# Token-sum stores on GpSimd's queue, the second batch's routing steps earlier, and up-factors through the fill buffers

## The chip, the cores and the metric

The kernel runs on one core of a Trainium2 chip. The metric is the device time of one execution in microseconds (us). The kernel is written with a tile framework: the source fixes the order of instructions on TensorE (PE), VectorE (DVE), ScalarE (ACT) and GpSimd (POOL) as it is written, and the framework orders the DMA issues of SyncE (SP) by a planner's due times. Every engine works through its own queue in order, so an instruction that waits holds up all behind it on its engine.

## The reference

Two batches of 1024 tokens with 1024 features go through a layer norm. A block-sparse linear layer (mask of 32 x 32 blocks) gives s. A LoRA mixture gives g: a plain linear layer, plus eight low-rank pairs weighted by a softmax that depends on the mean token of the batch. The output is x + s * g.

```python
xn = _layernorm(x)
s = einsum('bsk,nk->bsn', xn, weight * block_mask) + bias
base = einsum('bsi,oi->bso', xn, W_org)
q = einsum('bi,ki->bk', xn.mean(axis=1), Wq)
coeffs = softmax(einsum('bk,ek->be', q, lora_keys) / sqrt(128))
delta = einsum('be,bser,ero->bso', coeffs, einsum('bsi,eir->bser', xn, lora_down), lora_up)
out = x + s * silu(base + delta)
```

## The kernel before

Every float32 operand of a product is split in a high part (a cast on ACT) and a low part (a subtraction on DVE), and each product is three matmuls: high x high, high x low, low x high. A 128 x 512 output tile of a full-depth product is 24 matmuls (`gemm`, L425 to L427).

The order of work is this. Batch 0: the S product's first half, then the Y weights are made and the Y product's first half runs (phase `y00`), then its second half (phase `y01`, tiles 0 to 7, jobs in `jobs_c`). Then a stretch of *folds*: the Y weights of batch 1 are made by 16 folds (one per half and k tile) and stored to DRAM (`yu`), with the eight S tiles of batch 0's second half (`s_tile`) between them: 4, 4, 3, 3, 2 folds after S tiles 0 to 4. Last, batch 1's products are done by a Strassen-like scheme (`quad`, L1131), whose operand sums were prepared before.

A **fold** (`fold`) makes one 128 x 512 block of W_org^T + down x (coefficients * up). It loads `ds` (a down block) and `wo` (a W_org block) for the next fold (`y_prep`, L375 and L377), splits ds into `dhi` (ACT, L380) and `dlo` (DVE, L381), runs 12 matmuls into `psw` (`y_mul`, L389 to L391) and adds `wo` (DVE, L396). The scaled up-factors are the four `cut` tiles of one half: `scale_up(b, h)` loads four `us` tiles (L364), and multiplies each by the coefficients on ACT (L367, high) and DVE (L368, low). The second half's factors, `scale_up(1, 1)`, are made at the end of fold 7.

The **routing** of batch 1, `coeffs(1)`, gives four steps. steps[0] spreads the token sums by eight TensorE transposes (L297); steps[1] is the query (DVE, L321 and L325); steps[2] is the scores: a pair of small matmuls (L332), DVE's L334 to L337, and the exponential as a power on POOL (L339); steps[3] is the softmax's sum and division (DVE, L345 to L352), which gives the coefficients `c`. In the kernel before, jobs_c runs steps[0] and steps[1] after the seventh tile of y01 and its S weight, and the other two with `scale_up(1, 0)` after the eighth tile and its S weight.

Also in `jobs_c`: an S weight block per tile (`s_mul`: load of `ws`, L272, mask product on DVE, L274, cast on ACT, L277; `s_lo`: DVE, L282). S tile 0 needs the eighth of these blocks for its last three matmuls. And the **token sums** of batch 1: for each of four groups j, `wide_a` and `wide_b` normalize a block on DVE and form seven sums, which are stored to DRAM (`xv`), five DMAs a group: `ac` and `bd` of 512 KB, three more of 256 KB. They are put in `late_stores`, and `store_late` issues all that wait there from ACT's queue (L480); jobs_c calls it once a tile, between `s_mul` and `s_lo`.

A **fill** (`fill`, L984 to L986) loads one of these sums back into one third of `misc` (three buffers in turn, which held the query weights until steps[1] had read them), and splits it into `xw`, the operands of `quad`. Before, a fill follows the second and the fourth fold after S tiles 0 and 1.

Buffers that matter: `stage` has six 128 x 512 places, shared by ws, us, ds, wo and some sums; `cu` has five of 128 x 2 x 512, shared by the wide blocks of the sums and the cut tiles; `res` has three, each held until the output store that reads it has landed.

Of the kernel before, what the change touches and what calls it, by code (L numbers as in the profile page):

```python
# [9 lines left out]
F32 = mybir.dt.float32  # L10
# [7 lines left out]
P = 128  # L18
# [3 lines left out]
NKT = D // P  # L22
NH = 512
# [9 lines left out]
def kernel(  # L33
# [26 lines left out]
    nc = tc.nc  # L60
# [23 lines left out]
    stage = for_fold("stage", 2)  # L84
# [16 lines left out]
    misc = c0pool.tile([P, 3, NH], F32, name="misc")  # L101
# [254 lines left out]

    cu = {}

    def scale_up(b, h):
        cu[(b, h)] = []  # L360
        for c in range(4):
            t = cupool.tile([P, 2, NH], F32R, name="cut", tag="cu")
            st = stage.tile([P, NH], F32, name="us", tag="st", bufs=6)
            nc.sync.dma_start(st, up[c * P : (c + 1) * P, h * NH : (h + 1) * NH])  # L364
            s = csel[b][:, c : c + 1]
            hi = t[:, 0, :]
            nc.scalar.activation(hi, st, AF.Copy, scale=s)  # L367
            nc.vector.scalar_tensor_tensor(  # L368
                t[:, 1, :], st, s, hi.bitcast(F32), ALU.mult, ALU.subtract
            )  # L370
            cu[(b, h)].append(t)

    def y_prep(b, h, kt):
        ds = stage.tile([P, 4, P], F32, name="ds", tag="st", bufs=6)
        nc.sync.dma_start(ds, down[kt])  # L375
        ws = stage.tile([P, NH], F32, name="wo", tag="st", bufs=6)
        nc.sync.dma_start(ws, worgT[kt * P : (kt + 1) * P, h * NH : (h + 1) * NH])  # L377
        dhi = stage.tile([P, 4, P], F32R, name="dhi", bufs=2)
        dlo = stage.tile([P, 4, P], F32R, name="dlo", bufs=2)
        nc.scalar.copy(dhi, ds)  # L380
        nc.vector.tensor_tensor(dlo, ds, dhi.bitcast(F32), ALU.subtract)  # L381
        staged[(b, h, kt)] = dhi, dlo, ws

    def y_mul(b, h, kt):
        dhi, dlo, ws = staged[(b, h, kt)]
        u = cu[(b, h)]
        ps = ps_w.tile([P, NH], F32, name="psw", tag="psw")
        for c in range(4):
            nc.tensor.matmul(ps, lhsT=dhi[:, c, :], rhs=u[c][:, 0, :], start=c == 0, stop=False)  # L389
            nc.tensor.matmul(ps, lhsT=dhi[:, c, :], rhs=u[c][:, 1, :], start=False, stop=False)  # L390
            nc.tensor.matmul(ps, lhsT=dlo[:, c, :], rhs=u[c][:, 0, :], start=False, stop=c == 3)  # L391
        staged[(b, h, kt)] = ps, ws

    def y_sum(b, h, kt):
        ps, ws = staged[(b, h, kt)]
        nc.vector.tensor_tensor(ws, ws, ps, ALU.add)  # L396
# [18 lines left out]
    def open_gemm(b, i, w, c0=0, n=NH):  # L415

        ps = ps_acc.tile([P, NH], F32, name="acc_ps", tag="acc_ps")[:, :n]
        g, j = divmod(i, 4)
        xs = xg[(b, g)]
        cols = slice(j * P, (j + 1) * P)  # L420
        wc = slice(c0, c0 + n)

        def part(k0, k1):
            for kt in range(k0, k1):
                nc.tensor.matmul(ps, lhsT=xs[:, kt, 0, cols], rhs=w[:, kt, 0, wc], start=kt == 0, stop=False)  # L425
                nc.tensor.matmul(ps, lhsT=xs[:, kt, 0, cols], rhs=w[:, kt, 1, wc], start=False, stop=False)  # L426
                nc.tensor.matmul(ps, lhsT=xs[:, kt, 1, cols], rhs=w[:, kt, 0, wc], start=False, stop=kt == NKT - 1)  # L427

        return ps, part

    def gemm(b, i, w, c0=0, n=NH):
        ps, part = open_gemm(b, i, w, c0, n)
        part(0, NKT)
        return ps
# [40 lines left out]
    late_stores = []  # L475

    def store_late():

        while late_stores:
            nc.scalar.dma_start(*late_stores.pop(0))  # L480

    pending = []

    def flush():
        while pending:
            pending.pop(0)()

    def phase(kind, b, h, w, final, jobs):

        for i in range(TPB):  # L490
            t = b * TPB + i
            if final:
                res = stage_l.tile([P, NH], F32, name="res", tag="res", bufs=3)
                nc.sync.dma_start(res, x[t * P : (t + 1) * P, h * NH : (h + 1) * NH])
            flush()
            ps = gemm(b, i, w)
            if final:
                pending.append(J(final_evac, kind, b, h, i, ps, res))
            else:
                pending.append(J(tile_evac, kind, b, h, i, ps))  # L500
            for job in jobs(i):
                job()

    J = lambda f, *a: (lambda: f(*a))
# [98 lines left out]
    with tc.manual_schedule(engines={mybir.EngineType.PE, mybir.EngineType.DVE, mybir.EngineType.Activation, mybir.EngineType.Pool}):  # L603
# [256 lines left out]
        xv = dram.tile([4, P, 7, NH], F32, name="xv")  # L860
# [36 lines left out]
        def wide_norm(j, half):  # L897
            t = wide[j][2 * half]
            nc.vector.tensor_tensor(t, t, rows["mean"], ALU.subtract)
            nc.vector.scalar_tensor_tensor(  # L900
                t, t, 1.0, rows["rstd"], ALU.mult, ALU.mult, accum_out=xsum[:, j + 4 * half : j + 4 * half + 1]
            )

        def sub(o, a, b):
            nc.vector.tensor_tensor(o, a, b, ALU.subtract)

        def fresh():
            return stage.tile([P, NH], F32, name="xt", tag="st", bufs=6)
# [4 lines left out]
        def wide_b(j):  # L913

            wide_norm(j, 1)
            ac, (t1, t2), bd = wide[j]
            sub(t1, ac[:, 1], ac[:, 0])
            sub(t2, bd[:, 1], t1)
            sub(ac[:, 1], bd[:, 1], ac[:, 1])
            t4 = stash_p.tile([P, NH], F32, name="t4", tag="stash") if j == 0 else fresh()  # L920
            sub(t4, bd[:, 0], t2)
            late_stores.append((xv[j, :, 0:2, :], ac))
            late_stores.append((xv[j, :, 2:4, :], bd))
            for k, t in ((4, t1), (5, t2), (6, t4)):
                late_stores.append((xv[j, :, k, :], t))

        phase("y", 0, 0, y00, True, jobs_b)


        s1 = new_slot()  # L930
        steps = coeffs(1)

        def jobs_c(i):
            yield J(s_mul, s1, 1, i)
            yield J(store_late)
            yield J(s_lo, s1, 1, i)
            if i in (1, 3):
                yield J(wide_load, (i + 3) // 2, 0)
                yield J(wide_load, (i + 3) // 2, 1)
            if i < 6:  # L940
                yield J((wide_a, wide_b)[i % 2], 1 + i // 2)
            if i == 6:
                yield steps[0]
                yield steps[1]
            if i == 7:
                yield steps[2]
                yield steps[3]
                yield J(scale_up, 1, 0)

        phase("y", 0, 1, y01, False, jobs_c)  # L950


        folds = [(h, kt) for h in range(2) for kt in range(NKT)]

        def fold(n):
            h, kt = folds[n]
            if n + 1 < len(folds):
                y_prep(1, *folds[n + 1])
            store_late()
            y_mul(1, h, kt)  # L960
            flush()
            y_sum(1, h, kt)
            ps, ws = staged.pop((1, h, kt))
            late_stores.append((
                yu[:, :, 2 * h + kt // 4, kt % 4, :].rearrange("u p n -> p u n"),
                ws.rearrange("p (u n) -> p u n", n=P),
            ))
            if n == NKT - 1:
                scale_up(1, 1)

        xw = {}
        XV = (0, 2, 3, 4, 5, 1, 6)
# [15 lines left out]
        spare = []  # L988
        ORDER_X = (0, 3, 4, 1, 5, 2, 6)

        def s_tile(i):
            res = stage_l.tile([P, NH], F32, name="res", tag="res", bufs=3)
            nc.sync.dma_start(res, x[i * P : (i + 1) * P, NH:])
            store_late()
            flush()
            ps = gemm(0, i, s1)
            pending.append(J(final_evac, "s", 0, 1, i, ps, res))
# [6 lines left out]
        def unit_load(u, i):  # L1004
            kind, p = units[u]
            src = wu[p] if kind == "s" else yu[p].rearrange("p a j n -> p (a j n)")
            c = slice(2 * i * NH, 2 * (i + 1) * NH)
            nc.sync.dma_start(raw_flat[:, c], src[:, c])
# [45 lines left out]
        def fills(j, n):  # L1054
            for _ in range(n):
                fill(j, ORDER_X[filled[j]])
                filled[j] += 1

        for i, n in enumerate((4, 4, 3, 3, 2)):
            s_tile(i)  # L1060
            for k in range(n):
                fold(done)
                done += 1
                if i < 3 and (i == 2 or k in (1, 3)):
                    fills(0, 1)
                if i > 2 and (i == 4 or k):
                    fills(1, 1)
                if i in (2, 3):
                    early.pop(0)()
            if i == 0:  # L1070
                unit_load(0, 0)
                unit_load(0, 1)
# [198 lines left out]
```

## Time and profile before

| What | us |
|---|---|
| median of three runs | 464.17 (461.12 to 466.78) |
| the profiled execution's own time | 465.36 |
| its span, first to last instruction | 463.6 |
| mean granted TensorE clock | 0.982 of full speed |

The page divides the span in 40 slices. The row for the granted TensorE clock and that of the DMA engines' busy share are, in tenths:

```profile
PEclk9799999999999999997999999999999999999998
DMA  8995506587862497887878885754364237209103
```

A slice is 11.6 us, so y01 with its jobs is in slices 15 to 18, and the folds follow to slice 25. An engine's idle time costs something only where that engine sets the pace. A row of a group is read as: line, engine, operation, output <- inputs, count | busy us, mean ns of one | idle before it and who ended it. A releaser is inferred from semaphore events.

### The profile page before, as it was taken

Reading aid. Unit: us, or ns where it says so; the run is one execution under the profiler, and the core shown is the slowest. Engines: PE = TensorE matmul, PEld = TensorE weight load, DVE = VectorE, ACT = ScalarE, POOL = GpSimd, SP = SyncE. Lnnn points to the kernel's source line nnn. Section 1 sums busy time; section 2 is a strip of 40 time slices with the busy share of each in tenths; the row PEclk is TensorE's granted clock in tenths of the full one; section 3 lists DMA queues with packets and bytes.
Section 4 is the critical chain, followed back from the end, with each engine's and each line's share of the span. In section 5 each row is a group of like instructions: output and inputs, shape, how many; then the busy total and the mean of one; then the engine's idle time right before and its main releaser. Section 6 shows DMA issues by size and latency. Waiting matters only on the chain.

```text
span 463.6 us, 5733 instructions
## 1 busy us (share of the span) xinstructions
PE 446.5 (96%) x2047; PEld 366.5 (79%) x2047; DVE 304.8 (66%) x492; ACT 169.3 (37%) x277; POOL 48.6 (10%) x52
## 2 busy tenths in 40 slices
PE   7799999999999999996999899999999999999995
PEld 5689888888887888885888688877888888888884
DVE  6879778666775788856555875868474385455624
ACT  3566725354323132213314223248343332431510
POOL 3755310000010000001000000000030020002000
PEclk9799999999999999997999999999999999999998
DMA  8995506587862497887878885754364237209103
GB/s 268 391 326 190 165 24 198 187 258 254 303 229 92 166 324 263 285 294 257 259 224 265 249 286 169 249 176 149 106 136 138 90 93 181 90 13 209 51 1 113
DMA packets 48173, 89.52 MB, mean 193 GB/s; under 512 B 4752, under 2 KB 14992, under 8 KB 48144
## 3 DMA queue, kind: packets, MB, share of 16 engines
q1 hardware_dynamic: 32784, 70.28, 45.7%
q10 hardware_dynamic: 13632, 15.73, 10.0%
q0 software_dynamic: 1728, 3.15, 4.6%
q8 instruction: 16, 0.26, 0.2%
q14 instruction: 13, 0.11, 0.1%
HBM read 69.21 MB, written 19.92 MB: 192 GB/s over the span
## 4 chain that ended last, share of the span: by engine, by line
PE 76%; DVE 11%; DMA 6%; ACT 2%; issue 2%; ACTq 1%; POOL 0%; SPq 0%; DVEq 0%
PE acc_ps L1131 23%; PE py L1131 9%; PE acc_ps L427 8%; PE acc_ps L425 8%; PE acc_ps L426 8%; PE psw L391 6%; PE psw L389 6%; PE psw L390 6%; DMA ws<-in_wT_dram 3%; DMA raw<-in_x_dram 1%; DVE slot L544 1%; ACTq L480 1%; DMA us<-in_up_dram 1%; DMA xv<-bd 1%; DVE ws L274 1%
## 5 line engine op out<-in xcount | busy, mean ns | idle before, releaser
L1131 PE MATMUL acc_ps<-xw,ow 128*128 128x512 f32 x480 | 113.8, 393 | 0.4 <-ACT acc_ps L1162 0.4
L426 PE MATMUL acc_ps<-slot,xgrp 128*128 128x512 f32 (+1 forms) x288 | 106.9, 371 | 2.7 <-DVE slot L544 2.7
L425 PE MATMUL acc_ps<-slot,xgrp 128*128 128x512 f32 (+1 forms) x288 | 107.6, 374 | 0.1
L427 PE MATMUL acc_ps<-slot,xgrp 128*128 128x512 f32 (+1 forms) x288 | 106.6, 370 | 0.7 <-DVE xgrp L556 0.7
L1131 PEld LDWEIGHTS acc_ps<-xw,ow 128*128 128x128 f32 x480 | 90.0, 188 | 21.4 <-ACT acc_ps L1162 0.9
L426 PEld LDWEIGHTS acc_ps<-slot,xgrp 128*128 128x128 f32 x288 | 55.4, 192 | 12.2 <-DVE slot L544 3.6
L427 PEld LDWEIGHTS acc_ps<-slot,xgrp 128*128 128x128 f32 x288 | 55.3, 192 | 10.2 <-DVE xgrp L556 1.1
L425 PEld LDWEIGHTS acc_ps<-slot,xgrp 128*128 128x128 f32 x288 | 55.3, 192 | 9.1 <-DVE stash L439 0.3
L389 PE MATMUL psw<-cut,dhi 128*128 128x512 f32 x128 | 51.5, 403 | 3.8 <-ACT dhi L380 3.7
L391 PE MATMUL psw<-cut,dlo 128*128 128x512 f32 x128 | 51.4, 401 | 1.5 <-DVE dlo L381 1.5
L390 PE MATMUL psw<-cut,dhi 128*128 128x512 f32 x128 | 51.0, 398 | 0.0
L1131 PE MATMUL py<-xw,ow 128*128 128x512 f32 x192 | 46.9, 392 | 0.0
L1131 PEld LDWEIGHTS py<-xw,ow 128*128 128x128 f32 x192 | 36.1, 188 | 8.1
L1031 DVE TENSOR_TENSOR ow<-raw,ow 128x1024 fp32r<-128x1024 f32 (+1 forms) x32 | 34.5, 1088 | 9.8 <-ACT ow L1030 9.6
L380 ACT CAST dhi<-ds 128x512 fp32r<-128x512 f32 x32 | 19.8, 617 | 42.5 <-PE psw L390 22.6
L396 DVE TENSOR_TENSOR wo<-wo,psw 128x512 f32<-128x512 f32 x32 | 21.9, 685 | 17.1 <-PE psw L391 17.0
L389 PEld LDWEIGHTS psw<-cut,dhi 128*128 128x128 f32 x128 | 24.7, 193 | 9.7 <-ACT dhi L380 4.1
L1114 POOL DMA_DIRECT2D gate<-in_xT_dram x12 | 10.8, 932 | 199.9 <-DVE gate L1112 130.8
L391 PEld LDWEIGHTS psw<-cut,dlo 128*128 128x128 f32 x128 | 24.7, 193 | 8.2 <-DVE dlo L381 2.8
L1030 ACT CAST ow<-raw 128x1024 fp32r<-128x1024 f32 (+1 forms) x32 | 29.4, 940 | 2.0 <-DVE xw L986 2.0
L390 PEld LDWEIGHTS psw<-cut,dhi 128*128 128x128 f32 x128 | 24.8, 193 | 5.4
L381 DVE TENSOR_TENSOR dlo<-ds,dhi 128x512 fp32r<-128x512 f32 x32 | 21.9, 686 | 9.0 <-ACT dhi L380 9.0
(152 smaller groups left out, 450.0 us busy)
## 6 DMA issues: line engine op xcount, KB each, us to landing
ds<-in_down_dram SPq DMA_DIRECT2D x32, 256.0 KB, 3.5
wo<-in_worgT_dram SPq DMA_DIRECT2D x32, 256.0 KB, 3.8
raw<-in_x_dram SPq DMA_DIRECT2D x11, 512.0 KB, 5.9
res<-in_x_dram SPq DMA_DIRECT2D x16, 256.0 KB, 3.3
us<-in_up_dram SPq DMA_DIRECT2D x16, 256.0 KB, 3.7
out_dram<-res ACTq DMA_DIRECT2D x16, 256.0 KB, 2.9
raw<-in_wu_dram SPq DMA_DIRECT2D x8, 512.0 KB, 5.2
yu<-wo ACTq DMA_DIRECT2D x16, 256.0 KB, 3.7
```

The costliest lines, as they stand in the source:

```text
L380: nc.scalar.copy(dhi, ds)
L381: nc.vector.tensor_tensor(dlo, ds, dhi.bitcast(F32), ALU.subtract)
L389: nc.tensor.matmul(ps, lhsT=dhi[:, c, :], rhs=u[c][:, 0, :], start=c == 0, stop=False)
L390: nc.tensor.matmul(ps, lhsT=dhi[:, c, :], rhs=u[c][:, 1, :], start=False, stop=False)
L391: nc.tensor.matmul(ps, lhsT=dlo[:, c, :], rhs=u[c][:, 0, :], start=False, stop=c == 3)
L396: nc.vector.tensor_tensor(ws, ws, ps, ALU.add)
L425: nc.tensor.matmul(ps, lhsT=xs[:, kt, 0, cols], rhs=w[:, kt, 0, wc], start=kt == 0, stop=False)
L426: nc.tensor.matmul(ps, lhsT=xs[:, kt, 0, cols], rhs=w[:, kt, 1, wc], start=False, stop=False)
L427: nc.tensor.matmul(ps, lhsT=xs[:, kt, 1, cols], rhs=w[:, kt, 0, wc], start=False, stop=kt == NKT - 1)
L1030: nc.scalar.copy(o[:, a:b, 0], raw[:, a:b])
L1031: nc.vector.tensor_tensor(o[:, a:b, 1], raw[:, a:b], o[:, a:b, 0].bitcast(F32), ALU.subtract)
L1131: nc.tensor.matmul(ps, lhsT=o[:, a, wl, j, :], rhs=xw[j][:, m, xl, :], start=start and j == 0 and k == 0, stop=j == 3 and k == 2, skip_gro ...
```

## The change

1. The token-sum stores get a list of their own, `sum_stores`, which `store_sums` issues from POOL's queue directly after the sums of a group are formed. `jobs_c` no longer calls `store_late`; what is left in late_stores then (the last output tile of y00) goes out at the first fold.
2. steps[0] and steps[1] run ahead of the seventh S weight. steps[2] is put inside the last tile of y01, after four of its eight k steps (`split_at`). steps[3] and `scale_up(1, 0)` run ahead of the eighth S weight.
3. `scale_up(1, 1)` takes the three thirds of misc for three of its four loads; the turn of misc (`spare`) advances by three.
4. The second fill after S tiles 0 and 1 follows the third fold in place of the fourth.

In the built programs this moves on SP: the load of the eighth S weight behind the four loads of up-factors and two fill loads; the res load of S tile 2 from y01 to behind the fourth fold's loads; three of the second half's up-factor loads up to 8 places ahead of their old place, and three fill loads behind them. On ACT the 20 sum stores are gone; the eighth S weight's cast is behind the four L367. On DVE the eighth S weight's two operations are behind the four L368. On POOL the 20 stores stand between the last L152 and L339.

```diff
-    def scale_up(b, h):
+    def scale_up(b, h, homes=()):
         cu[(b, h)] = []
         for c in range(4):
             t = cupool.tile([P, 2, NH], F32R, name="cut", tag="cu")
-            st = stage.tile([P, NH], F32, name="us", tag="st", bufs=6)
+            st = homes[c] if c < len(homes) else stage.tile([P, NH], F32, name="us", tag="st", bufs=6)
...
+    sum_stores = []
+
+    def store_sums():
+
+        while sum_stores:
+            nc.gpsimd.dma_start(*sum_stores.pop(0))
+
+    split_at = {}
...
-            ps = gemm(b, i, w)
+            if (b, h, i) in split_at:
+                ps, part = open_gemm(b, i, w)
+                part(0, 4)
+                split_at[(b, h, i)]()
+                part(4, NKT)
+            else:
+                ps = gemm(b, i, w)
...
-            late_stores.append((xv[j, :, 0:2, :], ac))
-            late_stores.append((xv[j, :, 2:4, :], bd))
+            sum_stores.append((xv[j, :, 0:2, :], ac))
+            sum_stores.append((xv[j, :, 2:4, :], bd))
             for k, t in ((4, t1), (5, t2), (6, t4)):
-                late_stores.append((xv[j, :, k, :], t))
+                sum_stores.append((xv[j, :, k, :], t))
+            store_sums()
...
         def jobs_c(i):
+            if i == 6:
+                yield steps[0]
+                yield steps[1]
+            if i == 7:
+                yield steps[3]
+                yield J(scale_up, 1, 0)
             yield J(s_mul, s1, 1, i)
-            yield J(store_late)
             yield J(s_lo, s1, 1, i)
...
-            if i == 6:
-                yield steps[0]
-                yield steps[1]
-            if i == 7:
-                yield steps[2]
-                yield steps[3]
-                yield J(scale_up, 1, 0)
-
+
+        split_at[(0, 1, 7)] = steps[2]
         phase("y", 0, 1, y01, False, jobs_c)
...
             if n == NKT - 1:
-                scale_up(1, 1)
+                homes = [misc[:, (len(spare) + k) % 3, :] for k in range(3)]
+                spare.extend(homes)
+                scale_up(1, 1, homes)
...
-                if i < 3 and (i == 2 or k in (1, 3)):
+                if i < 3 and (i == 2 or k in (1, 2)):
                     fills(0, 1)
```

## The prediction

> **What bounds the kernel now.** I read the page's busy shares first, then PE's list of waits, then the table by stretches, then the chain of waits around each hole.
>
> ```profile
> PE 446.5 (96%) x2047; PEld 366.5 (79%) x2047; DVE 304.8 (66%) x492; ACT 169.3 (37%) x277; POOL 48.6 (10%) x52
> ```
>
> TensorE is the bound: 96% busy. From 150 to 210 us every 10 us stretch shows PE fully busy, so nothing the change moves there can gain by itself. Only holes can be won. PE's waits name two after 150 us that the change can reach:
>
> ```profile
> PE psw L389 <- ACT dhi L380: 3.7, 1, 3.7
> PE psw L391 <- DVE dlo L381: 1.5, 1, 1.5
> ```
>
> What each hole costs beyond the wait is in the stretches (busy PE, PEld, DVE, ACT, POOL, then the granted clock, DMA share, GB/s):
>
> ```profile
> 210.00:215.00 5.00, 2.12 (x10) 1.42 (x8) 2.37 (x7) 2.35 (x4) 1.65 (x1) 1.00 0.51 177
> 215.00:220.00 5.00, 4.23 (x10) 3.03 (x11) 3.49 (x6) 1.92 (x4) 0.00 (x0) 0.52 0.87 300
> 220.00:230.00 10.00, 10.00 (x41) 8.17 (x40) 5.40 (x9) 3.10 (x5) 0.00 (x0) 0.90 0.81 257
> 250.00:260.00 10.00, 8.28 (x35) 6.02 (x35) 8.49 (x13) 5.10 (x9) 0.00 (x0) 1.00 0.77 226
> ```
>
> After the first hole the clock is 0.52: matmuls follow each other every 0.43 us instead of 0.2275 until 222. After the second, shorter hole it stays 1.00. The first, in PE's own rows:
>
> ```profile
> 211.73 0.39 PE L427 MATMUL acc_ps<-slot,xgrp 128*128 128x512 f32 x1
> 215.77 0.79 PE L389 MATMUL psw<-cut,dhi 128*128 128x512 f32 x1 [3.65 <-ACT dhi L380]
> ...
> 222.07 0.39 PE L391 MATMUL psw<-cut,dlo 128*128 128x512 f32 x1
> ```
>
> At 0.2275 the first fold matmul would start at 211.96 and the 15th at 215.15; it starts at 222.07. **Hole one costs 6.92 us**: 3.81 of idling, 3.11 of half clock. For hole two I count starts from 254.40 to 260.19: 15 steps, 3.41 us at full pace, 5.79 taken: **2.38 us**. The chain of waits (start, length, what) tells why hole one exists:
>
> ```profile
> 202.39 0.70 DVE ws L274
> 203.12 0.33 ACT slot L277
> 203.49 0.57 ACTq L480
> 204.10 0.64 ACTq L480
> 204.78 1.18 ACTq L480
> 206.00 1.49 ACTq L480
> ...
> 208.12 0.62 ACT slot L277
> 208.76 0.69 DVE slot L282
> ...
> 210.07 1.66 POOL ex L339
> ```
>
> ACT issues the last five sum stores (L480) from 203.13 to 207.5, with SP's loads in flight (302 GB/s over 195 to 212). They hold up the cast L277 of the last S weight; DVE's L282 behind it holds up the scores; these give POOL's exponential, the coefficients, the factor casts L367 (212.65) and at last dhi.
>
> **The change, part by part** (line numbers of the kernel before).
>
> *Stores on POOL.* The 20 issues leave ACT; POOL has nothing else between 137 and 210. Only the fourth group stands in front of POOL's exponential. Nearest price: POOL's other DMA, L1114, mean 932 ns, 880 median. A store of 512 KB has as many packets: ACT's five stores of that window are 721 packets, 144 each, as the 12 gate DMAs have (1728/12). So five times 0.93: from 199.45 (the DVE row that finishes ac) POOL is busy to 204.1. [...] The row: the L1114 at 343.25 takes 0.87 us and lies inside a 1.23 us DVE L1031. DVE beside the stores has the same kind, two-input f32 operations, so I take 0.93. [...] From below: it can't be under 0.87 each, the shortest row.
>
> *Routing ahead.* steps[0] and steps[1] now precede the seventh S weight. PE's transposes for them sit at 199.92 as before and end at 200.95. DVE's two L321 and L325 took 1.63 us (204.38 to 206.01): now to 202.6. DVE is free then: it idled to 202.39 for the S weight's DMA. steps[2] sits after 12 of the last Y tile's 24 matmuls: 200.71 + 12 x 0.2275 = 203.4, 0.8 us after its operand, so PE does not wait. The seventh S weight: L274 to 203.3, L277 on a free ACT to 203.95, L282 to 204.65. Scores 0.6: 205.25. POOL, free since 204.1, runs L339 (1.65) to 206.95; sum, reciprocal, coefficients took 0.9: **L367 starts at 207.95 instead of 212.65**. The factor loads must be there: SP's four L364 rows stretch over 7.2 us (197.6 to 204.8) because the last waited for the store-delayed L282 (2.1 us) and one for an S weight's DMA (3.0); now one S weight fewer is ahead of them. The last two cut tiles take the places of ac and bd of the fourth group, so ACT's third and fourth L367 wait for those stores to land: issued at 199.45 and 200.4, landing by the gate row's median 5.5 at 205 and 205.9, by its maximum 8.8 at 208.3 and 209.2; needed at 209.4 and 210.1. Covered, by 0.9 at worst.
>
> *Last S weight behind the factors.* This is a new wait. Four L367/L368 took 3.49 us from the first L367: DVE is through at 211.45; then L274 0.69, L277 0.62, L282 0.69: high part 212.75, low part 213.45. Its load is issued when L282 frees its buffer, 204.7; with the window's S-weight landing 6.1 it is there at 210.8. S tile 0 on PE reaches this weight (its 22nd matmul) at 211.28. PE so waits 1.5 us, runs one matmul, waits 0.5, and the folds start at 213.95. dhi (L380) follows L277 by 213.5 if its load is there: issued after the first L368 (209.4), it lands at 212.9 with the page's median of 3.5 and at 214.3 with the 4.9 that it took at this place before (then the folds start at 215.0 and the gain is 1.0 less). I take 3.5, since the sum stores and fill loads that were in flight beside it now go out 3 us earlier. The gap of 1.5 equals hole two's 1.54, which left the clock at 1.00, so I take full pace: the 15th fold matmul starts at 213.95 + 14 x 0.2275 = 217.14. **Gain 4.9**. Bounds: 6.9 if nothing waited; 1.8 with the half clock (213.95 + 6.30 = 220.25).
>
> *Second half's factors in the fill buffers.* Hole two: ACT waits for these loads to 252.09 (L367), DVE is late with L368 at 252.85 and then works through its queue, so dlo comes at 259.1. In the change three of four loads go to misc, issued when a fill's L986 frees a third of it: two by 242.3, the last after L986 of fold 6, 243.67 + 0.7 + 0.6 = 245, landing (3.7) at 248.7. ACT then needs 1.4 and DVE ends at 250.85, 2.7 earlier, before fold 8 needs it (251.64, less hole one). Then L396 of fold 8 runs when PE ends it (254.4), followed by L986, L1016, L381: 257.6, where PE wants it at 257.55. **Gain 2.1**; bounds 0 and 2.4. Behind it SP issues three fill loads that wait for the L368 reads, and one wo and one ds stand behind them to about 250.5; they are used after 257.
>
> *At nothing.* The last first-half output store leaves with fold 0 (from 166 to about 213), and the res load that needs its buffer goes behind it to about 217; used at 254. The fill moved from the fourth to the third fold adds 0.6 ACT and 0.7 DVE ahead of the factors; DVE is half idle there (4.62 of 10 in 240 to 250). If that cover fails, up to 0.7.
>
> **Sum.** 4.9 + 2.1 = 7.0. The profiled execution took 465.36 with a span of 463.6: 458.4 and 456.6 after. The median of the runs, 464.17, is 1.2 lower than that execution: **457.2**. A measurement of this kernel tells about 1% (4.6 us) from no change.
>
> **Rivals.**
> - [...] Chance 0.10.
> - *One hole stays.* Either the gap of 2.0 in pieces still halves the clock (gain 1.8 + 2.1: 460.3), or hole two reappears behind the fill loads (4.9 + 0: 459.3). For it: the clock's limit lies somewhere between 1.54 and 3.65 us of idling here. Chance 0.20, 460.
> - *The holes move.* The last S weight or ds lands late (slack 0.6 and none, DMA near full), and PE waits as long at 211 as it did at 212: about 464. Chance 0.12.
> - *Other losses*, mainly loads behind SP's new waits: 0.03.
> - *Forecast*: 0.55, own range 455.5 to 458.8.
>
> Faster by over 1% takes in the forecast and a quarter of the second: 0.60. Within 1%: 0.25. Slower: POOL, and a part of the moved holes: 0.15. The range runs from 455.0 (both holes gone) to 464.2, which takes in the second rival and most of the third.
>
> **What would show it.** Right: L1114-like store rows near 0.9 on POOL, L339 near 205.3, L367 near 208, PE's longest wait near 211 at L425 to L427 under 2 us, granted clock 1.00 in 215 to 220, no wait at L391 near 252. Wrong: POOL rows over 1.6, a clock near 0.5 after 211, or a DMA releaser on L367 or on the last L274.

## The result, and the profile after

The kernel after takes 460.69 us (median of 22 runs, 457.56 to 462.08), the kernel before beside it 463.36 (22 runs, 460.39 to 467.02): a ratio of 0.9937, 95% interval 0.9914 to 0.9960. That is 2.7 us less; 7.0 were forecast. The change helps, by less than half of what was expected and less than the 1% named in the prediction.

The profiled execution has a span of 460.1 us against 463.6. Not all of these 3.5 us belong to the change. PE's last stall of over 0.3 us in the start-up (a matmul at L427) ends at 32.68 in the kernel after and at 34.07 in the kernel before, and up to there the two do the same work: 1.39 us is the start-up's own scatter (the granted clock was halved there for 6.8 us before and for 3.4 after). From that matmul to the end of PE's last one the kernel before takes 424.88 us and the kernel after 422.48, **2.40 us less**. I call this the body, and use it below, since it leaves out the start-up. A time of the kernel after is set beside one of the kernel before by adding 1.39.

Executions of one kernel also differ in the clock they were granted, and this limits what one profile can say. The 22 of the kernel after have means from 0.986 to 0.999, and the profiled one is the longest of them (462.08) at the lowest clock. The profiled execution of the kernel before has 0.982, where 77 others of that kernel have 0.984 to 0.999 (median 0.992).

In the kernel after, the lines from L984 on lie 16 higher (fills L1000 to L1002, mask product L1032, quad L1147), and the sum stores have their own line, L487. The two longest of PE's waits after 150 us:

```profile
PE acc_ps L425 <- ACT slot L277: 2.7, 1, 2.7
PE psw L391 <- DVE dlo L381: 0.8, 1, 0.8
```

Hole one is still there, with another releaser: not dhi, but the cast of the eighth S weight. Hole two is about half as long. The stretches (busy PE, PEld, DVE, ACT, POOL, then granted clock, DMA share, GB/s) show what each costs:

```profile
205.00:210.00 5.00, 5.00 (x23) 3.85 (x21) 3.61 (x8) 2.68 (x4) 0.08 (x1) 1.00 1.02 393
210.00:215.00 5.00, 2.27 (x6) 1.50 (x6) 2.61 (x5) 2.23 (x4) 0.00 (x0) 0.71 0.89 268
215.00:220.00 5.00, 5.00 (x15) 3.95 (x14) 2.52 (x5) 0.62 (x1) 0.00 (x0) 0.60 0.65 211
250.00:260.00 10.00, 9.22 (x40) 7.24 (x39) 9.93 (x15) 3.25 (x6) 0.00 (x0) 1.00 0.96 314
```

The clock still falls to 0.60 behind hole one, and DVE is busy for 9.93 of 10 us around hole two. Counted as in the prediction, by how much PE's starts lie behind a step of 0.2275 us each, hole one costs 5.9 us (before: 6.9) and hole two 1.0 (before: 2.3). The gains, 1.0 and 1.3, account for the body's 2.40. The chain of waits (start, length, what) of the kernel after names what keeps hole one open:

```profile
202.10 0.69 DVE slot L282
...
202.82 8.54 DMA ws<-in_wT_dram
...
211.38 0.70 DVE ws L274
...
212.11 0.63 ACT slot L277
...
212.78 0.80 PE acc_ps L425
```

L282 of the seventh S weight frees a buffer, SP issues the eighth's load into it at 202.82, and this load takes 8.54 us. Everything ahead of it in the forecast held. The rows of POOL (start, us, engine, line; the idle time and its releaser in brackets):

```profile
198.60 0.54 POOL L487 DMA_DIRECT2D xv<-ac  x1 [8.97 <-DVE ac L919]
199.20 0.54 POOL L487 DMA_DIRECT2D xv<-bd  x1
...
203.41 1.67 POOL L339 TENSOR_TENSOR ex<-ebase,sc 128x8 f32<-128x8 f32 x1 [2.01 <-DVE sc L337]
```

Each store of the fourth group costs POOL 0.54 us. L339 is not held up by them: POOL idles 2.01 us ahead of it.

### The profile page after: what moved, and what is told of

Its sections match the earlier page's. It is cut to its first block, busy times and chain, and to the rows that moved or that the text cites. A ratio compares the mean times of both kernels' runs of the same rounds, so it can differ in the third digit from the quotient of the medians.

```text
span 460.1 us, 5752 instructions
## 1 busy us (share of the span) xinstructions
PE 444.7 (97%) x2047; PEld 365.4 (79%) x2047; DVE 305.1 (66%) x492; ACT 169.3 (37%) x277; POOL 59.5 (13%) x72
## 4 chain that ended last, share of the span: by engine, by line
PE 85%; DVE 8%; DMA 4%; issue 1%; ACT 1%; SPq 0%; ACTq 0%; DVEq 0%
PE acc_ps L1147 23%; PE acc_ps L425 11%; PE acc_ps L426 11%; PE acc_ps L427 11%; PE py L1147 9%; PE psw L391 6%; PE psw L389 6%; PE psw L390 6%; DMA ws<-in_wT_dram 2%; DMA raw<-in_x_dram 1%; DVE slot L558 1%; DVE ramp L549 1%; DMA misc<-in_up_dram 1%; DVE st L144 1%; DVE xw L1002 1%
## 5 line engine op out<-in xcount | busy, mean ns | idle before, releaser
L1147 PE MATMUL acc_ps<-xw,ow 128*128 128x512 f32 x480 | 113.6, 393 | 0.4 <-ACT acc_ps L1178 0.4
L425 PE MATMUL acc_ps<-slot,xgrp 128*128 128x512 f32 (+1 forms) x288 | 107.4, 373 | 2.8 <-ACT slot L277 2.7
L427 PE MATMUL acc_ps<-slot,xgrp 128*128 128x512 f32 (+1 forms) x288 | 106.4, 369 | 0.7 <-DVE xgrp L570 0.7
L1147 PEld LDWEIGHTS acc_ps<-xw,ow 128*128 128x128 f32 x480 | 90.0, 188 | 21.3 <-ACT acc_ps L1178 0.8
L425 PEld LDWEIGHTS acc_ps<-slot,xgrp 128*128 128x128 f32 x288 | 54.8, 190 | 12.3 <-ACT slot L277 3.1
L427 PEld LDWEIGHTS acc_ps<-slot,xgrp 128*128 128x128 f32 x288 | 55.0, 191 | 10.2 <-DVE xgrp L570 1.1
L391 PE MATMUL psw<-cut,dlo 128*128 128x512 f32 x128 | 50.9, 397 | 0.8 <-DVE dlo L381 0.8
L1147 PE MATMUL py<-xw,ow 128*128 128x512 f32 x192 | 46.9, 392 | 0.0
L1147 PEld LDWEIGHTS py<-xw,ow 128*128 128x128 f32 x192 | 36.1, 188 | 8.1
L396 DVE TENSOR_TENSOR wo<-wo,psw 128x512 f32<-128x512 f32 x32 | 22.0, 686 | 18.6 <-PE psw L391 18.5
L391 PEld LDWEIGHTS psw<-cut,dlo 128*128 128x128 f32 x128 | 24.5, 192 | 6.7 <-DVE dlo L381 1.2
L1192 DVE TENSOR_TENSOR py<-py,s 128x512 f32<-128x512 f32 x8 | 5.6, 698 | 30.7 <-ACT s L1154 30.7
```

The source lines that it names most:

```text
L1147: nc.tensor.matmul(ps, lhsT=o[:, a, wl, j, :], rhs=xw[j][:, m, xl, :], start=start and j == 0 and k == 0, stop=j == 3 and k == 2, skip_gro ...
```

## The experiments

Twelve kernels were run, each timed beside the kernel before (whose medians there were 462.78, 463.45 and 463.55 for the first four, the next four and the last four kernels in the order e1 to e4, p1, p2, e5, e6, then e7, e8, p3, p4); a ratio is to those runs. "Hole one" and "hole two" are the microseconds by which PE's starts fall behind full pace in 203 to 224 and in 240 to 262, in the profiled execution.

| kernel | median us | ratio to before (95%) | body | hole one | hole two |
|---|---|---|---|---|---|
| before | 463.36 | 1 | 424.88 | 6.9 | 2.3 |
| after | 460.69 | 0.9937 (0.9914 to 0.9960) | 422.48 | 5.9 | 1.0 |
| e1_own | 458.36 | 0.9891 (0.9852 to 0.9930) | 420.01 | 1.5 | 2.1 |
| e2_ahead | 459.85 | 0.9948 (0.9921 to 0.9976) | 420.25 | 1.8 | 2.4 |
| e3_early | 458.63 | 0.9924 (0.9894 to 0.9953) | 421.09 | 3.6 | 1.3 |
| e4_hold | 460.84 | 0.9945 (0.9925 to 0.9966) | 421.70 | 1.0, and 2.7 of filler | 1.6 |
| p1_pool | 460.13 | 0.9940 (0.9913 to 0.9967) | 421.52 | 4.2 | 1.8 |
| p2_homes | 461.40 | 0.9954 (0.9926 to 0.9982) | 423.70 | 6.5 | 1.7 |
| e5_thin | 457.36 | 0.9869 (0.9823 to 0.9915) | 420.19 | 1.5 | 2.4 |
| e6_mask | 457.95 | 0.9894 (0.9863 to 0.9925) | 418.16 | 2.0 | 0.0 |
| e7_best | 458.68 | 0.9891 (0.9857 to 0.9926) | 417.68 | 1.6 | 0.0 |
| e8_earlymask | 456.80 | 0.9870 (0.9840 to 0.9900) | 419.01 | 2.2 | 0.1 |
| p3_undo1 | 460.02 | 0.9931 (0.9905 to 0.9956) | 423.11 | 5.4 | 1.8 |
| p4_nosteps | 459.73 | 0.9935 (0.9903 to 0.9968) | 420.19 | 3.8 | 0.4 |

The intervals are about 3 us wide, so the medians tell the first group (about 460) from the best (457 to 458), not neighbours. The holes of single executions are what tells the mechanisms apart: the wait, its releaser, and whether the clock fell behind it. But body and holes are those of one execution, and some of these are extremes of their kernel: the longest for after (of 22), e3_early (of 8), e8_earlymask (of 4) and p3_undo1 (of 10), the shortest for e2_ahead (of 14) and e6_mask (of 6). A body therefore does not rank a kernel.

### e1_own: the eighth S weight loaded into a place of its own

```
-        st = stage.tile([P, NH], F32, name="ws", tag="st", bufs=6)
+        if kt == 7:
+            st = raw_flat[:, 3 * D : 3 * D + NH]
+        else:
+            st = stage.tile([P, NH], F32, name="ws", tag="st", bufs=6)
```

> The kernel after, but the eighth S weight (the last one of tile 0's S matmuls) is loaded into a free stretch of the raw-score buffer instead of a ring buffer, so its load no longer waits for L282 and goes out some microseconds before the crowded stretch; it is still cast and split behind the factors on DVE and ACT. Theory 1 (the load's landing made the gap): in the kernel after DVE was free for L274 1.69 us before the load landed (211.36), so L274 now starts near 209.7, PE waits at L425 1.0 to 1.2 us instead of 2.73, the granted clock stays near 1.00 in 210 to 220, and the time falls by 1.7 + about 3 = 4 to 5 us against the kernel after. Theory 2 (the landing matters, but any gap of a microsecond at this place halves the clock): PE's wait falls to about 1.1, the clock still shows 0.5 to 0.7 after 211, gain 1.5 to 2. Theory 3 (the order on DVE and ACT made the gap, and the late landing was beside it): PE's wait stays over 2.3 us, gain under 0.5.

The lines shift by 3 here (L425 is L428, L391 is L394). PE's waits, then two stretches:

```profile
PE psw L394 <- DVE dlo L384: 1.5, 1, 1.5
PE acc_ps L1150 <- ACT s L1157: 0.8, 1, 0.8
PE acc_ps L428 <- ACT slot L280: 0.8, 1, 0.8
```

```profile
210.00:215.00 5.00, 4.78 (x20) 3.73 (x21) 3.99 (x7) 2.35 (x4) 0.00 (x0) 1.00 0.88 298
215.00:220.00 5.00, 5.00 (x24) 4.14 (x23) 3.42 (x6) 1.86 (x3) 0.00 (x0) 1.00 0.91 267
```

The wait at the S tile falls from 2.73 to 0.8 and the clock stays at 1.00, with the order on DVE and ACT as in the kernel after: theory 1 holds, theories 2 and 3 fall. Hole one gives 4.4 us. But the wait at hole two grows from 0.8 to 1.5 and one near 300 appears: the body gains 2.5 on the kernel after, not the 4 to 5 expected.

### e5_thin: why the load takes 8.5 us

```
-            sum_stores.append((xv[j, :, 0:2, :], ac))
+            q = slice(0, P if j < 3 else 16)
+            sum_stores.append((xv[j, q, 0:2, :], ac[q]))
...
-            nc.sync.dma_start(st, xv[j, :, XV[m], :])
+            nc.sync.dma_start(st, xv[min(j, 2), :, XV[m], :])
```

> The kernel after with the fourth group's five sum stores cut to an eighth of their bytes (16 of 128 partitions); the second half of the outputs that depend on this group is not the reference's, and the fourth group's later loads read the third group's sums, so that every load moves the same bytes as before. The order and the number of the instructions stay. Theory C (the eighth S weight's load lands late because the stores move 1.8 MB beside it): its landing falls from 8.5 us to 5 or less, PE's wait at L425 from 2.73 to about 1.0 (DVE, which comes free at 209.7, sets it then). Theory Q (it lands late because it stands behind SP's own six loads of 256 KB): it stays at 7 us or more, and PE's wait over 1.5.

The kernel leaves out seven eighths of the fourth group's sums.

The DMA issues of 198 to 212 (count, KB each, median us from issue to landing), first of the kernel after, then of e5_thin:

```profile
xv<-ac POOLq DMA_DIRECT2D x1, 512.0 KB, 7.2
misc<-xv SPq DMA_DIRECT2D x2, 256.0 KB, 8.6
ws<-in_wT_dram SPq DMA_DIRECT2D x1, 256.0 KB, 8.5
```

```profile
misc<-xv SPq DMA_DIRECT2D x2, 256.0 KB, 6.1
ws<-in_wT_dram SPq DMA_DIRECT2D x1, 256.0 KB, 4.9
```

The same load at the same place in SP's order lands after 4.9 us when the stores' 1.8 MB shrink to an eighth. Theory C holds and theory Q falls: the stores in flight beside it, not SP's own loads ahead of it, made the difference of 3.6 us. It is not the queue of POOL as such: beside stores that go out from ACT (p3_undo1 below) the load took 7.2. PE's wait at L425 is 0.8, the clock 1.00, hole one 1.5, as in e1_own. In the kernel after they share DMA engines that are full (a share of 1.02 at 393 GB/s in 205 to 210).

### e2_ahead and e3_early: the eighth S weight ahead of the factors again

```
 # e2_ahead (in jobs_c); e3_early has this and the place of e1_own
+            yield J(s_mul, s1, 1, i)
+            yield J(s_lo, s1, 1, i)
             if i == 7:
                 yield steps[3]
                 yield J(scale_up, 1, 0)
-            yield J(s_mul, s1, 1, i)
-            yield J(s_lo, s1, 1, i)
```

> The kernel after, but in the last Y tile's slot the cast and split of the eighth S weight stand ahead of the coefficients and of the factor casts again, as in the kernel before; the load is as late as in the kernel after. Theory 1 (landing): DVE's and ACT's queues now wait for the load (issue 202.8, landing 6 to 8.5 us, so 209 to 211.4) before they touch the factors: L367 starts at 210 to 212 instead of 206.0, dhi comes 4 to 6 us later, and the hole of the kernel before is back: slower than the kernel after by 3 to 6 us, about the kernel before. Theory 3 (order): with the weight ahead of the factors PE no longer waits at L425, and the factors are ready in time: faster than the kernel after by 2 to 5 us.

> Both edits: the eighth S weight has a place of its own, so it lands early, and is cast and split ahead of the factors. Theories 1 and 2: nothing waits for the load, the eighth S weight is done near 204.5, L367 starts 0.7 us later than in the kernel after (206.7), PE runs through tile 0 of S without a wait, and the first fold matmul waits at most 0.5 us for dhi near 210.5; the clock stays near 1.00: 5 to 6 us faster than the kernel after, about 455. If the S load was not the limit but the factors' chain or the ds load behind it: a wait of 2 us or more at the first fold (L389) takes its place, and the gain is under 2.

In e2_ahead I expected the load to stay late, and it didn't. The six places of `stage` are handed out in the order of the program, so with the eighth weight first, its load goes out with the seventh's, and the fourth factor load takes the place that L282 frees. The chain of waits of e2_ahead, then of e3_early, where the factors have a place more and it is the first fold's ds that comes last:

```profile
199.64 0.69 DVE slot L282
...
200.37 7.63 DMA us<-in_up_dram
```

```profile
202.88 0.69 DVE slot L285
...
203.60 8.71 DMA ds<-in_down_dram
```

Three kernels, one place in the chain, three different loads: 8.54, 7.63 and 8.71 us. What costs is the ring place that opens beside the stores; the order only chooses who gets it. The price differs: PE's longest wait is 1.1 us in e2_ahead and 1.54 in e3_early, where it also halved the clock (0.69 in 215 to 220), so hole one is 1.8 and 3.6. The medians (459.85 and 458.63) don't follow this: the profile of e2_ahead is its shortest execution, that of e3_early its longest. Both are faster than the kernel before; the first theory's "3 to 6 us slower" for e2_ahead rested on the wrong load and fails.

### e4_hold: filler in the gap

```
+            if i == 0:
+                ps, part = open_gemm(0, i, s1)
+                part(0, 7)
+                hold = ps_w.tile([P, 4, P], F32, name="hold", tag="psw")
+                for _ in range(12):
+                    nc.tensor.matmul(hold, lhsT=ones_r, rhs=ones_r.unsqueeze(1).to_broadcast([P, 4, P]),
+                                     start=True, stop=True)
+                part(7, 8)
...
```

> The kernel after, with 12 matmuls of constant operands (their result is not used) ahead of the eighth step of S tile 0, where PE waited 2.73 us: 12 x 0.2275 = 2.73 us of work in the gap. The load and the order stay. Clock theory: PE is busy through the gap, the granted clock stays near 1.00 in 210 to 220, and the time falls by the half clock's share, about 3 us, against the kernel after. Rival (the clock falls for another reason at this place, or the steps of 0.43 us are operand waits): the steps stay at 0.43 until about 219, and the time is the same or up to 1 us longer.

```profile
210.00:215.00 5.00, 4.54 (x20) 3.20 (x19) 2.57 (x4) 2.02 (x4) 0.00 (x0) 1.00 0.89 296
215.00:220.00 5.00, 5.00 (x24) 4.12 (x23) 3.88 (x6) 1.46 (x3) 0.00 (x0) 1.00 0.82 261
```

The load is as late as before (8.8 us), but the clock stays at 1.00: the steps of 0.43 us in the kernel after are the clock, not operands. Hole one with the filler costs 3.7 instead of 5.9. Of these 2.2 us hole two takes 0.6 back, and the rest is lost in a wait near 304 to 311 (0.8 us at L1157): the body gains 0.8 and the median nothing. The clock theory holds, its 3 us do not.

### p1_pool, p2_homes, p3_undo1, p4_nosteps: the parts alone

p1_pool is the kernel before with the stores on POOL; p2_homes the kernel before with `homes` in scale_up(1, 1) and the fills after folds `k in (1, 2)`; p4_nosteps has both of these, thus the change without the reordering; p3_undo1 is the kernel after with the stores back in `late_stores` and `store_late` between `s_mul` and `s_lo`.

> The kernel before with the first part of the change alone: the sum stores go out from POOL's queue; the order of the routing steps, the place of the S weights and the factors' homes stay as before. Theory S (ACT's issues of the last five stores, 203.5 to 207.5, were the cause of hole one): the last cast L277 starts near 204 instead of 208.1, the factors' first cast near 208.6 instead of 212.65, PE waits for dhi under 1.5 us instead of 3.7, the clock stays near 1.00: 5 to 6 us faster than the kernel before, so the reordering of the change was not needed for hole one and cost what the stores had won. Theory L (the landing of a load in the full stretch 200 to 211 sets the end whatever ACT does): a wait for a DMA of 7 to 9 us stands in the chain and PE waits 2 to 3 us: 1 to 2 us faster, as the whole change.

> The kernel before with the last part of the change alone: three of the second half's four factor loads go to the fill buffers and one fill moves from the fourth fold to the third. Hole one stays as in the kernel before (PE idle 3.7 us, half clock). If hole two's gain in the kernel after belongs to this part: the wait at L391 near 257 falls from 1.5 to about 0.8 and the time by 1.1 to 1.4 us. Rival (the gain at hole two came because PE arrived later or earlier there, not from the loads): the wait stays at 1.5 and the time is the same within 0.5 us.

> The kernel after with its first part undone: the sum stores are issued from ACT again, between the casts of the S weights, all else as in the kernel after. ACT then issues the fourth group's stores (4 us in the kernel before) ahead of the factors' casts: L367 starts near 208 to 210 instead of 206, the eighth S weight's cast behind it near 213 to 214, and PE waits over 3.5 us at L425: slower than the kernel after by 1 to 3 us, about the kernel before. Rival (the stores' issue is hidden now that the scores come earlier): within 1 us of the kernel after.

> The kernel after without its second part: stores on POOL and the factors' homes as in the kernel after, the routing steps and the eighth S weight in the order of the kernel before. From the run of the stores alone (body 3.4 us shorter than the kernel before, hole two's wait 1.6) and of the homes alone (1.2): if the two add up, 4.5 us faster than the kernel before, 2 faster than the kernel after, and the reordering is a loss. If PE's earlier arrival at hole two takes up the homes' gain: about 3.4, still 1 faster than the kernel after. If the reordering is worth something: slower than the kernel after.

PE's waits at the two holes, of p1_pool, p2_homes, p3_undo1 and p4_nosteps:

```profile
PE psw L391 <- DVE dlo L381: 1.9, 2, 1.6
PE psw L389 <- ACT dhi L380: 1.7, 1, 1.7
```

```profile
PE psw L389 <- ACT dhi L380: 4.1, 1, 4.1
PE psw L391 <- DVE dlo L381: 1.4, 1, 1.4
```

```profile
PE acc_ps L425 <- ACT slot L277: 3.5, 1, 3.5
PE psw L391 <- DVE dlo L381: 1.5, 1, 1.5
```

```profile
PE psw L389 <- ACT dhi L380: 1.4, 1, 1.4
PE psw L391 <- DVE dlo L381: 0.3, 1, 0.3
```

- The stores alone cut PE's wait at hole one from 3.7 to 1.7. The body gains 3.4, more than the whole change's 2.4. Theory S gave 5 to 6, because it left out that a wait of 1.7, with one of 0.3 close behind, can halve the clock (0.78 in 215 to 220).
- The homes alone give 1.2 in the body: 0.6 at hole two, where the wait stays at 1.4, and most of the rest from a half clock of 3.4 us where the kernel before had 6.8. Neither expectation fits well. With the stores (p4_nosteps) hole two's wait falls to 0.1 (the 0.3 listed lies at hole one, 213.82), where the stores alone left 1.6. So hole two needs the earlier loads, and the body gains 4.7.
- The change without its reordering has a body 2.3 us shorter than with it. The medians (459.73 and 460.69, ratios 0.9935 and 0.9937) do not tell the two apart; so what the runs show is that the reordering brought no measurable gain. Part of the 2.3 us is half clock, which lasted 6.8 us in the one profile and 3.4 in the other.
- Undoing the stores in the kernel after makes PE's wait 3.5 as expected (now the last factor's cast waits for the store of bd, which holds the place of its cut tile and takes 7.86 us, and the eighth S weight stands behind it), but the half clock is shorter (0.76 instead of 0.60 in 215 to 220), so hole one is 5.4 and not longer than the kernel after's 5.9. The time is that of the kernel after: here the rival's number came out, for another reason than the rival's.

### e6_mask, e8_earlymask, e7_best: hole two, and all together

e6_mask is e1_own with this; e8_earlymask is e3_early with it:

```
-                if i in (2, 3):
+                if (i, k) != (2, 0) and i >= 2 and early:
                     early.pop(0)()
```

e7_best is e8_earlymask, with the first fold's ds at `raw[:, 4]`.

> The kernel after with the eighth S weight in a place of its own (as in the run e1_own), and the six mask and sum operations of the first unit one fold later each, so that none of them (L1035, 1.22 us) stands ahead of the ninth fold's low part L384 on DVE. Theory D (hole two is DVE's queue): the wait of 1.54 us at L394 near 250 falls to 0.4 or less, and the time by about 1.2 us against e1_own, to about 457. Theory G (what is won at hole two is given back behind it): the wait falls, but waits near 300 and after grow by about as much, and the time is that of e1_own within 0.5. Theory M (hole two is the landing of the factors' loads): the wait stays over 1.2.

> As e3_early (the eighth S weight in a place of its own and ahead of the factors), with the first unit's mask and sum operations one fold later. Hole one as in e3_early: the first ds load is the one that waits for the ring, PE waits about 1.5 us for dhi. In e3_early the clock was halved for some 3.5 us after this wait, while a wait of the same 1.54 us near 250 left it at 1.00 in three kernels. If a wait of 1.5 us always halves the clock at this place: granted clock near 0.7 in 215 to 220 again. [...]

> All that the runs so far point to, on top of the kernel after: the eighth S weight in a free stretch of the raw-score buffer and ahead of the factors, the first fold's down weights (ds) in another free stretch of it, so that their load goes out ahead of the factors' loads, and the first unit's mask and sum operations one fold later. If the late landing of whichever load waits for a ring buffer in 200 to 211 is all there is to hole one: no wait over 0.5 us at the S tile or the first fold, clock 1.00 in 210 to 220, no wait at L391's place near 250; against e6_mask another 1.5 to 2 us of the body, about 456. Rival: the next load in the ring (wo or the second ds) takes the late place and PE waits over 1 us in the first or second fold; then the time is that of e6_mask.

Of PE's waits after 150 us, of e6_mask (lines shifted by 3), then of e7_best (by 6; both at hole one):

```profile
PE acc_ps L428 <- ACT slot L280: 1.2, 1, 1.2
PE acc_ps L1150 <- ACT s L1157: 0.6, 1, 0.6
```

```profile
PE psw L395 <- ACT dhi L386: 0.6, 1, 0.6
PE psw L397 <- DVE dlo L387: 0.3, 1, 0.3
```

The edit moves the first unit's six mask and sum operations one fold later each, so that a product of 1.22 us no longer stands ahead of the ninth fold's low part. This removes hole two altogether (theory D; M falls, and G nearly: the waits near 300 did not grow). The bodies are 6.7 and 7.2 us shorter than the kernel before's. e7_best's one profile reaches the forecast gain, with other means, but lies only 0.5 us below e6_mask's where 1.5 to 2 were expected, and its median, 458.68 (454.78 to 459.34), is 4.9 us below the kernel before beside it. Of the versions run, e8_earlymask has the lowest median of those that compute the whole reference: 456.80 in four executions, ratio 0.9870 (0.9840 to 0.9900), 6.8 us below the kernel before beside it; its interval does not meet that of the kernel after (0.9914 to 0.9960).

e8_earlymask and e3_early make the same wait at the same place, and differ in the clock. A row of PE and two stretches of 3.41 us of e3_early, then of e8_earlymask:

```profile
213.06 0.50 PE L392 MATMUL psw<-cut,dhi 128*128 128x512 f32 x1 [1.54 <-ACT dhi L383]
211.24:214.65 3.41, 1.87 (x8) 1.03 (x7) 1.05 (x2) 1.83 (x3) 0.00 (x0) 1.00 0.94 309
214.65:218.06 3.41, 3.41 (x10) 2.64 (x9) 2.63 (x5) 0.62 (x1) 0.00 (x0) 0.50 0.79 258
```

```profile
211.69 0.50 PE L392 MATMUL psw<-cut,dhi 128*128 128x512 f32 x1 [1.69 <-ACT dhi L383]
208.10:211.51 3.41, 1.90 (x9) 1.25 (x7) 1.14 (x2) 1.21 (x2) 0.00 (x0) 1.00 0.98 329
211.51:214.92 3.41, 3.23 (x13) 2.38 (x14) 2.36 (x4) 1.46 (x4) 0.00 (x0) 1.00 0.87 273
```

1.54 us of waiting halved the clock, 1.69 us did not. The stretches are cut at whole multiples of 3.413 us from the changes of each trace's own clock (last section): e3_early's wait falls into one of them, e8_earlymask's is split, 1.51 and 0.18. So at this length it is not the wait alone that decides.

## Why the prediction was right or wrong

- **What bounds the kernel: right.** Only the two holes were to be won, and less their two holes all the bodies are 415.5 to 416.7 us; waits of under 1 us near 300 make up most of what differs.
- **Stores on POOL: right, and cheaper.** 0.54 us each instead of 0.93, below the 0.87 that was called the least; POOL is through at 201.4. The first rival (0.10, and "POOL" among the slower cases) rested on a price of a store far above these, which no run shows. DVE ran two-input float32 operations beside these stores, and of all 20 the longest took 0.77. At 1.6 each, the sign named for being wrong, five from 199.45 on would have held POOL to 207.45, about as long as ACT's issues lasted before (207.5).
- **Routing ahead: its times right, its worth not.** L339 at 203.41 + 1.39 = 204.8 (forecast 205.3), the first L367 at 206.01 + 1.39 = 207.4 (207.95). But p4_nosteps does as well without it: what the routing gained, the eighth S weight's load lost.
- **The eighth S weight's load: the step that failed.** The prediction saw that L282 opens its place, and its time (202.82 + 1.39 = 204.2; forecast 204.7), but gave the load "the window's S-weight landing 6.1". It took 8.54. The 6.1 was measured in the kernel before, where these loads go out ahead of the last stores; in the kernel after this load goes out 1.4 us after the last of them, with all five still in flight, because the change issues the stores earlier and the load later. (For ds, a few lines on, the prediction did count the stores' new place; for this load it did not.) e5_thin shows the cause, e1_own that nothing else kept PE's wait above 0.8. The signs named for being wrong came: a DMA releaser on the last L274 (1.69 us) and on one L367 (0.22), and a half clock behind 211. The chance for it stood in the third rival, "the holes move": the right mechanism, at 0.12. Its price, 464, was too high: the wait was 2.73 us where it had been 3.65, and hole two shrank.
- **Full clock behind the gap: failed.** It was argued from one wait of 1.54 us that left the clock alone. With 2.73 us, inside the span that the second rival had left open (1.54 to 3.65), it halves; and e3_early, p1_pool and p4_nosteps show it halved after 1.4 to 1.7. It costs about 2.2 of the kernel after's 5.9 us (e4_hold). Together these two steps leave 1.0 of the forecast 4.9.
- **Hole two: right in direction, 1.3 instead of 2.1.** The third factor load was issued at 245.04 + 1.39 = 246.4 instead of 245, and DVE, which got its third factor only at 249.13, then worked without a pause to the dlo at 255.46. The prediction counted L1016's 1.2 us into this queue (L1032 now), but took L396 as waiting for PE; it was DVE that was behind:

```profile
249.13 0.75 DVE L368 SCALAR_TENSOR_TENSOR cut<-misc,c,cut 128x512 fp32r<-128x512 f32 x1 [3.05 <-ACT cut L367]
...
254.32 1.22 DVE L1032 TENSOR_TENSOR raw<-raw,m_sb 128x1024 f32<-128x1024 f32 x1
255.46 0.69 DVE L381 TENSOR_TENSOR dlo<-ds,dhi 128x512 fp32r<-128x512 f32 x1
```

e6_mask shows that with L1032 out of this place no hole is left.
- **The sum: failed too, unseen.** 4.9 + 2.1 took the holes as independent. They are not: where hole one shrank to 1.5 to 1.8 (e1_own, e2_ahead, e5_thin), hole two grew to 2.1 to 2.4, as much as in the kernel before. In e1_own the third factor's cast moved forward by 4.23 us (244.15 instead of 248.38) and PE's arrival by 4.99 (250.27 instead of 255.26); from that factor's DVE row to dlo it is 6.3 us in both. So PE came earlier to a queue that did not shorten. Had the S weight landed in time, the gain would have been about 5, not 7.0 (e1_own: 4.9 in the body, 4.4 in the medians).
- **The number: luck in part.** 460.69 is close to the second rival's 460. Its half clock did come, but behind a longer wait than it assumed, and its 1.8 and 2.1 were 1.0 and 1.3. Besides, the forecast of 457.2 started from three executions (464.17); the median of 22 is 463.36. And 3.1 of the 6.9 us to be won at hole one were half clock of one execution, whose clock, 0.982, was below that of the 77 others on record.

## What to carry to other kernels

When a change moves loads or stores, give the moved one the landing time of the stretch it moves into, with the new neighbours in it, not the one it had: here 6.1 became 8.5 because 1.8 MB of stores were in flight beside it. A ring of buffers makes one load the last; changing the order only changed which (8.54, 7.63 and 8.71 us in three kernels here), and a place outside the ring, where one is free, takes the load out of the contest (e1_own: PE's wait fell from 2.73 us to 0.8). And add the gains of two stalls only after asking what the second one waits for: if that is another engine's queue, time won at the first is handed over at the second until that queue is shortened too (hole two grew from 1.0 us in the kernel after to 2.1 in e1_own, and was 0.0 in e6_mask).

## What was not expected of the hardware

- The clock after a wait. At the first hole it was halved after single waits of 4.1, 3.7, 3.5, 2.7 and 1.54 us (p2_homes, before, p3_undo1, after, e3_early) and after 1.7 and 1.4 with 0.3 close behind (p1_pool, p4_nosteps), and not after 1.69 (e8_earlymask); at hole two waits of 1.4 to 1.6 us left it at 1.00 in seven kernels.
- The steps of the clock. In each of the 14 traces, all changes of the granted clock lie whole multiples of 3.413 us apart (before: at 17.23, 24.05, 215.20 and 222.03), so time can be cut there in steps of 3.413 us. Between 100 and 440 us, a step at full clock in which PE idled 1.69 us or more (p4_nosteps; 2.0 to 3.3 in p1_pool, after, before, p2_homes, p3_undo1) was followed by half clock; one with 1.51 or less was not; of three with 1.54, e3_early's was, those of e1_own and e5_thin at hole two were not. At the first hole the half clock lasted a second step where PE idled 0.57 or 0.66 us in the first (before, after), and one step where it idled 0.26 or less. No run here sets the phase of the steps, so that the split of 1.51 and 0.18 us saved e8_earlymask is argued, not shown.
- Five stores, 1.8 MB, issued from POOL within 3 us landed after 7.2 to 10.3 us, and loads of 256 KB issued among or just behind them after 7.6 to 8.8; with an eighth of those bytes a load took 4.9.
